# Division by shared row sums and the output projection at later ticks in a four-layer attention kernel

## The chip, the cores and the metric

The kernel runs on one core of one Trainium2 chip, in one launch, in fp32 throughout. The metric is device time in microseconds. The time before is the median of three runs, 2481.57 us (2477.61 to 2482.33).

## The reference, cut to what matters

The input is `x` of shape (4, 512, 32, 32): four images, each 512 channels by 1024 positions. Four layers follow each other. Layer 0 is attention with 8 heads of 64 channels, layer 1 is linear attention, layer 2 is attention with one head of 512 channels, layer 3 is attention with 4 heads of 128 channels after a group norm. Layers 0 and 3 are what the change touches. Both do this:

```python
attn = softmax(q @ k.T * scale)      # over 1024 keys
res  = attn @ v                      # per head
out  = res @ Wo.T + bo + x
```

The softmax is computed here without subtracting a maximum: exps are summed per row, the exps multiply the values as they are, and the product is divided by the row sum afterwards. That division, and the projection by `Wo` behind it, are what is moved.

## The kernel before, in words

`plain_path` is the path that runs. It goes layer by layer and image by image. For each image of layers 0 and 3, `project_qkv` makes q, k and v, and `attention` (L895) does the rest, with its output projection running on into the next image's `project_qkv`.

**Steps of `attention`.** The queries are halved into `qb` = 0, 1 (512 positions each). The channels are four chunks `g` = 0..3 of 128, which in layer 0 hold two heads each (`pair` is true) and in layer 3 one head. A step `(qb, g, i)` treats a part of the keys: 128 in layer 0 (8 steps per `g`), 256 in layer 3 (4 steps per `g`). `scores(n)` (L919) multiplies q and k into a PSUM tile `sc` (L924 in layer 0, L929 in layer 3), ScalarE takes the exp into a tile `pt` (L934; there are four `pt` buffers, so an exp waits until the values and the addition of the step four back are through), and VectorE adds the exps of a chunk into `sum` (L940 for the first two steps, L943 for each later one, L950 folds the halves in layer 3). `values(n - 2)` (L952) multiplies the exps of two steps back with v into PSUM tiles `acc` (L960 in layer 0, L975 in layer 3). At the last step of a chunk the product is copied into the tile `ot` (L970 and L971 in layer 0, where two PSUM tiles are joined; L983 in layer 3). `ot` has one buffer, `acc` has four.

**Shared row sums.** Chunks are grouped (`shared`, L912 to L916). In layer 0 the groups are two chunks each, three groups per image; the last two chunks of an image have their sums made singly by `sum_rows` (L985, matmuls at L992). In layer 3 the groups are the four chunks of `qb` = 0 and the first three of `qb` = 1. When a group is complete, `sum_shared` (L1004) multiplies its `sum` tiles with ones (L1011), so that each head's row sums lie in a few partitions, takes one reciprocal for the whole group (L678, with two reductions at L681), and sends the quotients by DMA to a small DRAM tile (L1023) and from there, broadcast over partitions, into the tile `rds` (L1026; two transfers in layer 0, one in layer 3). `normalise` (L1035) multiplies one chunk of `ot` with its quotients on VectorE (L1039) and adds the output bias to `x` on ScalarE (L1042).

**The output projection.** `project_out` (L1050) multiplies `ot` with `wo` by seven block products instead of eight. Its lead is the first product, a ScalarE copy of that PSUM tile (L1091), and four additions and subtractions of blocks of `ot` on VectorE (`sum_inputs`, L686 to L689). It returns three further pieces, `second`, `third` and `fourth`, each with two products (four matmuls of 128x256 each, all at L1072) and additions into `x` or the scratch tile `ou` (L1080, L1102). `second` accumulates onto the PSUM tile of the lead; `fourth` accumulates onto the two tiles of `third`. In layer 3 each finished block of `x` is stored by a DMA (L1085).

**What sets the order.** TensorE's order is the program's order, written out by hand. On the other engines a planner orders the instructions by its own model of costs; `tc.issue_after(ins)` tells it to place what is issued inside behind `ins`, and `soon()` gives a higher priority. Within the loop of steps, `later` is a first-in-first-out list of `[ticks, function]`: `tick()` (L651), called after each `values`, lowers all counts by one and runs what has come to zero from the front of the list. Layer 0 has two steps per turn of the loop (`per` = 2): two `scores`, then two times values and a tick.

Before the change, in layer 0 a complete group gets one entry due after one tick, which does `sum_shared` and straight after it `normalise` of both chunks. In layer 3 `sum_shared` is called ahead of the last `values` of the group, and `normalise` right behind that. `project_out`'s lead and three pieces for `qb` = 0 are due after 5, 6, 7, 8 ticks in layer 0 and after 4, 5, 5, 6 in layer 3. For `qb` = 1, whose last chunk isn't shared, the counts are one (layer 0) or two (layer 3) lower, and the change leaves them alone.

Of the kernel before, what the change touches and what calls it, by code (L numbers as in the profile page):

```python
# [15 lines left out]
ALU = mybir.AluOpType  # L16
# [458 lines left out]
def plain_path(ctx: ExitStack, tc: tile.TileContext, d: dict, out: bass.AP, count):  # L475
# [11 lines left out]
    nc = tc.nc  # L487
# [11 lines left out]
    def acc_tile():  # L499
        return ps_acc.tile([P, TB], F32, tag="acc", name="acc")  # L500

    def two_tile(name):
        return ps_sc.tile([P, 2, TB], F32, tag="sc", name=name)

    def row_tile(name):
        return work.tile([P, TB], F32, tag="row", bufs=3, name=name)

    def pt_tile(name):
        return work.tile([P, 2, TB], F32, tag="pt", bufs=4, name=name)

    def sum_tile(name):
        return work.tile([P, 2, TB], F32, tag="sum", bufs=2, name=name)

    def many_tile(name):
        return work.tile([P, NC, TB], F32, tag="many", name=name)
# [129 lines left out]
    later, pieces = [], []  # L645
# [5 lines left out]
    def tick():  # L651
        for item in later:
            item[0] -= 1
        while later and later[0][0] <= 0:
            later.pop(0)[1]()
# [13 lines left out]
    def flush():  # L669
        while later:  # L670
            later.pop(0)[1]()
        while pieces:
            pieces.pop(0)()


    def invert(rd, ps):

        nc.vector.reciprocal(rd, ps)  # L678
        n, m = next(unit), rd.shape[0]
        for i, t in enumerate((ps, rd)):  # L680
            closing[:] = [nc.vector.tensor_reduce(tops[:m, i, n : n + 1], t, AX.X, ALU.max).ins]  # L681
# [213 lines left out]
    def attention(b, q, key, v, heads, scale, wo, os, bo, hooks={}, last=False, end=None, plain=False):  # L895
# [6 lines left out]
        pair = hd < P  # L902
# [5 lines left out]
        pts, accs, rds, outs, ots, exps = {}, {}, {}, {}, {}, []  # L908
# [5 lines left out]
        else:  # L914
            shared = [[(qb, g) for g in range(NC - qb)] for qb in range(NTB)]
        group_of = {u: us for us in shared for u in us}  # L916
        parts_of = {}

        def scores(n):  # L919
            qb, g, i = steps[n]  # L920
            ps = two_tile("sc")
            if pair:
                for h, s in itertools.product(range(2), range(2)):
                    nc.tensor.matmul(  # L924
                        ps[half(h), s, :], lhsT=key(g, i)[half(s), half(h)],
                        rhs=q[qb][half(s), g, :], start=True, stop=True,
                    )
            for s in range(0 if pair else 2):
                nc.tensor.matmul(  # L929
                    ps[:, s, :], lhsT=key(g, 2 * i + s), rhs=q[qb][:, g, :], start=True, stop=True  # L930
                )
            pt = pt_tile("pt")
            with soon():
                exps.append(nc.scalar.activation(pt, ps, AF.Exp, scale=scale).ins)  # L934
            pts[n] = pt
            us = group_of.get((qb, g), [])
            if i == 1:
                acc = many_tile("sum")[:, :2, :] if pair and g % 2 and us else sum_tile("sum")
                accs[qb, g] = acc
                nc.vector.tensor_tensor(acc, pts[n - 1], pt, ALU.add)  # L940
            elif i > 1:
                acc = accs[qb, g]
                nc.vector.tensor_tensor(acc, acc, pt, ALU.add)  # L943
            if i == nsteps - 1 and not pair:
                total = acc[:, 0, :]
                if us:
                    if g == 0:
                        parts_of[qb] = many_tile("sums")
                    total = accs[qb, g] = parts_of[qb][:, g, :]
                nc.vector.tensor_tensor(total, acc[:, 0, :], acc[:, 1, :], ALU.add)  # L950
# [53 lines left out]
        def sum_shared(us):  # L1004

            heads = [(u, s) for u in us for s in range(2 if pair else 1)]
            n = P // 4
            ps = acc_tile()
            for k, (u, s) in enumerate(heads):
                acc = accs[u]  # L1010
                nc.tensor.matmul(  # L1011
                    ps[k * n : (k + 1) * n, :], lhsT=ones[:, :n],
                    rhs=acc[:, s, :] if pair else acc, start=True, stop=True,
                )
            m = len(heads) * n
            rd = row_tile("rd")
            invert(rd[:m], ps[:m])
            spread = work.tile([P, NC, TB], F32, tag="rds", name="rds")

            home = dram.tile(  # L1020
                [len(heads), TB], F32, tag=f"quotients{len(heads)}", bufs=2, name="quotients"
            )
            nc.sync.dma_start(home, rd[0:m:n])  # L1023
            for s in range(2 if pair else 1):
                to = spread[half(s) if pair else slice(0, P)]
                nc.sync.dma_start(  # L1026
                    to[:, : len(us), :],
                    home[s :: 2 if pair else 1].partition_broadcast(to.shape[0]),
                )
            for i, u in enumerate(us):  # L1030
                accs.pop(u)
                rds[u] = spread[:, i, :]
            return us

        def normalise(qb, g):  # L1035
            rd = rds.pop((qb, g))
            o = ots[qb][:, g, :]
            source = outs.pop((qb, g))[0] if (qb, g) in outs else o
            nc.vector.tensor_tensor(o, source, rd, ALU.mult)  # L1039
            xv = x[:, g, bass.ts(qb, TB)]  # L1040
            with tc.issue_after(exps[-1]):
                nc.scalar.activation(xv, xv, AF.Identity, bias=bo[:, g : g + 1])  # L1042
# [108 lines left out]
        for m in range(0, len(steps) + 2, per):  # L1151
            for n in range(m, m + per):
                if n < len(steps):
                    scores(n)
            for n in range(m, m + per):
                if n >= 2:
                    qb, g, i = steps[n - 2]
                    final = i == nsteps - 1

                    us = group_of.get((qb, g))  # L1160
                    closes = us and (qb, g) == us[-1]
                    if final and not pair and closes:
                        sum_shared(us)
                    elif final and not pair and not us:
                        sum_rows(qb, g)
                    values(n - 2)
                    tick()
                    if final and pair and closes:
                        later.append(
                            [1, lambda us=us: [normalise(*u) for u in sum_shared(us)]]  # L1170
                        )
                    elif final and pair and not us:
                        later.append([1, lambda qb=qb, g=g: (sum_rows(qb, g), normalise(qb, g))])
                    elif final and closes:
                        for u in us:
                            normalise(*u)
                    elif final and not pair and not us:
                        normalise(qb, g)
                    if n - 2 == len(steps) - 1 and end is not None:
                        flush()  # L1180
                        end_program(qb)
                    elif final and g == NC - 1 and plain and qb == NTB - 1:
                        later.append([2 * per + 1, lambda qb=qb: project_out_plain(qb)])
                    elif final and g == NC - 1:
                        rest = []
                        lead, *others = (4, 5, 6, 7) if pair else (2, 3, 3, 4)

                        wait = (1 if pair else 2) if us else 0
                        later.append(
                            [lead + wait, lambda qb=qb, rest=rest: rest.extend(project_out(qb))]  # L1190
                        )
                        for i in others:
                            later.append([i + wait, lambda rest=rest: rest.pop(0)()])
                if parts:
                    parts.pop(0)()
                if n in hooks:
                    parts.extend(hooks[n]())
# [444 lines left out]
    with tc.manual_schedule(engines={mybir.EngineType.PE}):  # L1642
# [95 lines left out]
        for b in range(B):  # L1738
# [20 lines left out]
            pair = lambda t, i: t[:, 2 * i : 2 * i + 2, :]  # L1759
# [145 lines left out]
```

## Time and profile before

| | |
|---|---|
| runs, median of 3 | 2481.57 us (2477.61 to 2482.33) |
| profiled execution, its own time | 2483.01 us |
| its span, first to last instruction | 2481.2 us |
| mean granted TensorE clock | 0.998 |
| layer 0, attention of image 0 (79 to 212 us): PE, DVE, ACT busy | 128.22, 99.62, 70.35 of 133 us |
| layer 3, attention of image 0 (1704 to 1830 us): PE, DVE, ACT busy | 126.00, 64.36, 45.24 of 126 us |
| L1039 divisions by `rds`, 128x512, two in a row | 1.29 us |
| L943 additions of exps, 128x1024 | 1.23 us each |
| transfers `quotients`, `rds` | 24 of 256 KB and 4 of 1024 KB for `rds` |

A row of the timeline gives the start in us from the span's start, the duration in us, the engine, the line, the operation, the tiles written and read, and how many instructions in a row it merges. Where the engine was idle before it, the idle time and what ended it follow in brackets. PE rows are pipelined: one row's end overlaps the next one's start, so waits on PE are better read from start to start. Each fp32 matmul shows as two rows.

### The profile page before, as it was taken

Reading aid. Unit: us, or ns where it says so; the run is one execution under the profiler, and the core shown is the slowest. Engines: PE = TensorE matmul, PEld = TensorE weight load, DVE = VectorE, ACT = ScalarE, POOL = GpSimd, SP = SyncE. Lnnn points to the kernel's source line nnn. Section 1 sums busy time; section 2 is a strip of 40 time slices with the busy share of each in tenths; the row PEclk is TensorE's granted clock in tenths of the full one; section 3 lists DMA queues with packets and bytes.
Section 4 is the critical chain, followed back from the end, with each engine's and each line's share of the span. In section 5 each row is a group of like instructions: output and inputs, shape, how many; then the busy total and the mean of one; then the engine's idle time right before and its main releaser. Section 6 shows DMA issues by size and latency. Waiting matters only on the chain.

```text
span 2481.2 us, 24717 instructions
## 1 busy us (share of the span) xinstructions
PE 2449.9 (99%) x10122; PEld 1222.9 (49%) x10122; DVE 1530.0 (62%) x1822; ACT 708.9 (29%) x867; POOL 252.5 (10%) x240
## 2 busy tenths in 40 slices
PE   9999999999999999999999999999999999999998
PEld 4444544454445443554644546446556455555644
DVE  3577567856775678657676684763554454455344
ACT  1444244414441444211120301102320421332132
POOL 4001100110011000300302112021011001002000
PEclk9999999999999999999999999999999999999999
DMA  5000020002000301010101002110010001000001
GB/s 183 10 10 9 5 77 10 10 5 77 10 9 5 128 18 60 0 72 0 68 0 68 5 0 85 51 68 18 26 38 34 17 30 51 1 34 30 1 22 44
DMA packets 28064, 86.25 MB, mean 35 GB/s; under 512 B 2396, under 2 KB 10076, under 8 KB 25384
## 3 DMA queue, kind: packets, MB, share of 16 engines
q1 hardware_dynamic: 27944, 84.61, 9.5%
q8 instruction: 81, 1.33, 0.2%
q14 instruction: 39, 0.32, 0.0%
HBM read 58.23 MB, written 25.32 MB: 34 GB/s over the span
## 4 chain that ended last, share of the span: by engine, by line
PE 90%; DVE 5%; DMA 3%; ACT 1%; issue 1%; SPq 0%; DVEq 0%; ACTq 0%
PE acc L706 20%; PE acc L827 11%; PE acc L975 9%; PE sc L929 9%; PE acc L834 8%; PE acc L1072 6%; PE acc L1300 6%; PE sc L924 6%; PE acc L960 5%; PE acc L1261 2%; DVE sum L943 2%; DMA rds<-quotients 2%; DVE rd L678 2%; PE feat L641 1%; ACT pt L934 1%; PE acc L641 1%
## 5 line engine op out<-in xcount | busy, mean ns | idle before, releaser
L934 ACT ACTIVATE pt<-sc 128x1024 f32<-128x1024 f32 x384 | 381.1, 1024 | 605.6 <-PE sc L929 333.7
L943 DVE TENSOR_TENSOR sum<-sum,pt 128x1024 f32<-128x1024 f32 x256 | 314.4, 1228 | 149.3 <-ACT pt L934 139.0
L960 PE MATMUL acc<-pt,v 64*64 64x512 f32 x2048 | 260.1, 594 | 0.0
L924 PE MATMUL sc<-q,k 64*64 64x512 f32 x2048 | 254.1, 595 | 3.5 <-ACT pt L934 3.5
L975 PE MATMUL acc<-pt,v 128*128 128x512 f32 x512 | 240.8, 594 | 0.0
L929 PE MATMUL sc<-q,k 128*128 128x512 f32 x512 | 239.8, 593 | 0.0
L694 POOL TENSOR_TENSOR ws<-wqkv 128x256 f32<-128x256 f32 (+1 forms) x40 | 40.7, 1017 | 1332.4 <-PE acc L992 560.8
L706 PE MATMUL acc<-t,ws 128*128 128x512 f32 x384 | 173.9, 593 | 0.0
L975 PEld LDWEIGHTS acc<-pt,v 128*128 128x128 f32 x512 | 96.6, 190 | 125.3 <-issue 124.4
L940 DVE TENSOR_TENSOR sum<-pt 128x1024 f32<-128x1024 f32 x64 | 77.9, 1217 | 124.4 <-ACT pt L934 124.4
L929 PEld LDWEIGHTS sc<-q,k 128*128 128x128 f32 x512 | 96.8, 190 | 112.8 <-issue 90.8
L924 PEld LDWEIGHTS sc<-q,k 64*64 64x64 f32 x2048 | 78.8, 134 | 147.6 <-issue 130.4
L960 PEld LDWEIGHTS acc<-pt,v 64*64 64x64 f32 x2048 | 79.7, 133 | 143.5 <-issue 140.4
L706 PEld LDWEIGHTS acc<-t,ws 128*128 128x128 f32 x384 | 72.5, 190 | 86.6 <-issue 84.7
L678 DVE RECIPROCAL rd<-acc 128x512 f32<-128x512 f32 (+1 forms) x24 | 80.5, 3353 | 39.2 <-PE acc L1011 39.2
L745 ACT COPY v<-acc 128x512 f32<-128x512 f32 x24 | 14.1, 587 | 288.0 <-PE acc L827 288.0
L1072 PE MATMUL acc<-ot,wo 128*128 128x256 f32 x336 | 80.5, 382 | 7.5 <-DVE ot L1039 7.5
L827 PE MATMUL acc<-ws,t 128*128 128x256 f32 x384 | 87.3, 379 | 0.0
L834 PE MATMUL acc<-qs,w 128*128 128x512 f32 x192 | 86.6, 593 | 0.0
L834 PE MATMUL acc<-q,ln 128*128 128x512 f32 x192 | 85.8, 593 | 0.0
L745 ACT COPY q<-acc 128x512 f32<-128x512 f32 x40 | 23.5, 587 | 208.5 <-PE acc L706 208.5
L1072 PEld LDWEIGHTS acc<-ot,wo 128*128 128x128 f32 x336 | 62.8, 190 | 38.2 <-issue 23.5
(326 smaller groups left out, 3514.6 us busy)
## 6 DMA issues: line engine op xcount, KB each, us to landing
home<-x SPq DMA_DIRECT2D x8, 2048.0 KB
x<-home SPq DMA_DIRECT2D x8, 2048.0 KB
out<-x SPq DMA_DIRECT2D x32, 256.0 KB
x<-in_x SPq DMA_DIRECT2D x3, 2048.0 KB
rds<-quotients SPq DMA_DIRECT2D x24, 256.0 KB
rds<-quotients SPq DMA_DIRECT2D x4, 1024.0 KB
wo<-in_wo SPq DMA_DIRECT2D x3, 1024.0 KB
w<-in_w SPq DMA_DIRECT2D x1, 3072.0 KB
```

The lines of the kernel that those rows point to most:

```text
L678: nc.vector.reciprocal(rd, ps)
L706: nc.tensor.matmul(ps, lhsT=w[:, m, :], rhs=x[:, m, :], start=start, stop=stop, skip_group_check=True)
L827: nc.tensor.matmul(ps[:, bass.ts(r, C // 2)], lhsT=x[:, m, bass.ts(2 * o + r, P)], rhs=w[:, m, :], start=(start and r == 0), stop=stop, sk ...
L834: nc.tensor.matmul(ps, lhsT=x[:, m, bass.ts(o, P)], rhs=w[:, m, :], start=start, stop=stop, skip_group_check=True,)
L924: nc.tensor.matmul(ps[half(h), s, :], lhsT=key(g, i)[half(s), half(h)], rhs=q[qb][half(s), g, :], start=True, stop=True,)
L929: nc.tensor.matmul(ps[:, s, :], lhsT=key(g, 2 * i + s), rhs=q[qb][:, g, :], start=True, stop=True)
L934: exps.append(nc.scalar.activation(pt, ps, AF.Exp, scale=scale).ins)
L943: nc.vector.tensor_tensor(acc, acc, pt, ALU.add)
L960: nc.tensor.matmul(outs[qb, g][r][half(s), :], lhsT=v[i // 2][half(r), i % 2, g * P + s * hd : g * P + (s + 1) * hd], rhs=pt[half(r), s, : ...
L975: nc.tensor.matmul(outs[qb, g][0], lhsT=v[j // 2][:, j % 2, bass.ts(g, P)], rhs=pt[:, s, :], start=(j == 0), stop=(j == NT - 1),)
L1072: nc.tensor.matmul(ps[i][:, bass.ts(o, n)], lhsT=w[:, m, bass.ts(o, P)], rhs=t[:, m, :], start=(start and m + o == 0), stop=(stop and m == ...
L1300: nc.tensor.matmul(ps[i, o], lhsT=w[m][:, bass.ts(o, P)], rhs=t[m], start=(start and m == 0), stop=(stop and m == 3), skip_group_check=True,)
```

## The change

`sum_shared` no longer leads straight into `normalise`. A new function, `normalise_shared`, does the divisions and bias additions of a group, placed behind the latest addition of exps that has been issued at that time (the new list `adds` holds them all). In layer 0 `sum_shared` stays due after one tick and the divisions are due after five. In layer 3 the divisions are due three ticks after the group is complete instead of at once. `project_out` for `qb` = 0 is due after 6, 7, 8, 8 ticks in layer 0 instead of 5, 6, 7, 8, and in layer 3 all four pieces are due after 4 ticks instead of 4, 5, 5, 6.

```diff
-        parts_of = {}
+        parts_of, adds = {}, []
...
-                nc.vector.tensor_tensor(acc, pts[n - 1], pt, ALU.add)
+                adds.append(nc.vector.tensor_tensor(acc, pts[n - 1], pt, ALU.add).ins)
             elif i > 1:
                 acc = accs[qb, g]
-                nc.vector.tensor_tensor(acc, acc, pt, ALU.add)
+                adds.append(nc.vector.tensor_tensor(acc, acc, pt, ALU.add).ins)
...
-            return us
+
+        def normalise_shared(us):
+
+            with tc.issue_after(adds[-1]):
+                for u in us:
+                    normalise(*u)
...
                     if final and pair and closes:
-                        later.append(
-                            [1, lambda us=us: [normalise(*u) for u in sum_shared(us)]]
-                        )
+                        later.append([1, lambda us=us: sum_shared(us)])
+                        later.append([5, lambda us=us: normalise_shared(us)])
...
                     elif final and closes:
-                        for u in us:
-                            normalise(*u)
+                        later.append([3, lambda us=us: normalise_shared(us)])
...
-                        lead, *others = (4, 5, 6, 7) if pair else (2, 3, 3, 4)
-
-                        wait = (1 if pair else 2) if us else 0
+
+
+                        if pair:
+                            lead, *others = (6, 7, 8, 8) if us else (4, 5, 6, 7)
+                        else:
+                            lead, *others = (4, 4, 4, 4) if us else (2, 3, 3, 4)
                         later.append(
-                            [lead + wait, lambda qb=qb, rest=rest: rest.extend(project_out(qb))]
+                            [lead, lambda qb=qb, rest=rest: rest.extend(project_out(qb))]
                         )
                         for i in others:
-                            later.append([i + wait, lambda rest=rest: rest.pop(0)()])
+                            later.append([i, lambda rest=rest: rest.pop(0)()])
```

## The prediction

> **What bounds the kernel now.** I began with the page's busy table: TensorE is the bound, and little is left on it.
>
> ```profile
> PE 2449.9 (99%) x10122; PEld 1222.9 (49%) x10122; DVE 1530.0 (62%) x1822; ACT 708.9 (29%) x867; POOL 252.5 (10%) x240
> ```
>
> So an edit pays only if PE waits less. The second view was the list of waits, kept to PE (total us, times, longest):
>
> ```profile
> PE acc L1072 <- DVE ot L1039: 7.5, 4, 2.0
> PE acc L992 <- DVE sum L943: 4.8, 4, 1.4
> ...
> PE sc L924 <- ACT pt L934: 3.5, 8, 0.6
> PE acc L992 <- DVE ot L971: 2.4, 4, 0.6
> PE acc L1072 <- DVE oi L687: 1.1, 4, 0.3
> ```
>
> L1039 is the division that the change moves. Counts of four are one per image, all in layer 0's attention. Third, the timeline of VectorE after the third shared group of image 0, where the quotients come back by DMA:
>
> ```profile
> 192.10 2.55 DVE L943 TENSOR_TENSOR sum<-sum,pt 128x1024 f32<-128x1024 f32 x2
> 197.77 1.29 DVE L1039 TENSOR_TENSOR ot<-ot,rds 128x512 f32<-128x512 f32 x2 [3.13 <-DMA rds<-quotients]
> 198.98 1.22 DVE L943 TENSOR_TENSOR sum<-sum,pt 128x1024 f32<-128x1024 f32 x1
> ...
> 200.72 1.22 DVE L943 TENSOR_TENSOR sum<-sum,pt 128x1024 f32<-128x1024 f32 x1
> 201.85 1.22 DVE L940 TENSOR_TENSOR sum<-pt 128x1024 f32<-128x1024 f32 x1
> 202.99 0.68 DVE L971 TENSOR_TENSOR ot<-ot,acc 128x512 f32<-128x512 f32 x1
> ```
>
> VectorE stands 3.13 us in front of the division with two additions behind it whose exps were finished long before. PE in the same stretch:
>
> ```profile
> 199.67 1.04 PE L960 MATMUL acc<-pt,v 64*64 64x512 f32 x8
> 202.08 1.04 PE L992 MATMUL acc<-sum,ones 64*64 64x512 f32 x2 [1.38 <-DVE sum L943]
> 203.73 0.66 PE L992 MATMUL acc<-sum,ones 64*64 64x512 f32 x3 [0.60 <-DVE ot L971]
> ```
>
> Fourth, granted clock by stretch (start:end, length, then busy us of PE, PEld, DVE, ACT, POOL, then PEclk):
>
> ```profile
> 205.00:207.00 2.00, 2.00 (x16) 0.79 (x12) 1.97 (x3) 0.59 (x1) 1.59 (x2) 0.50 0.00 0
> 454.00:456.00 2.00, 2.00 (x24) 0.67 (x20) 1.97 (x3) 1.01 (x2) 2.00 (x3) 1.00 0.02 4
> ```
>
> After that stall image 0 runs at half clock; image 1, at the same place, doesn't. Images 0 and 2 took 13.80 and 13.86 us from L992 to the first L706, images 1 and 3 both 12.17. Last, layer 3 (from 1705 us), by the same timeline, has no PE stall at all.
>
> **What the Trainium skill says.** "TensorE: Matmul & The Clock Gate", Architectural detail: ScalarE and VectorE are strict FIFO. The trace agrees: ready additions stood 3.13 us behind L1039. Same page, Part 1, the HAM clock gate: an idle window of about 3.4 us, free-running, halves the clock. The trace agrees roughly: 0.50 for about 3.4 us, in two images of four with the same stalls. "DMA: Bandwidth & Descriptors", Anatomy of one DMA: about 2 us fixed, mostly completion. The quotients' two chained transfers took 6.7 us here (issue 191.08, division 197.77). "PSUM — Partial Sum Buffer", PSUM bank collisions: a bank that another engine reads must be guarded against a matmul's write; no row of before has PE stopped by it.
>
> **The change part by part.** I measure stalls start to start: 16 rows of 64x512 take 1.72 us when nothing stops them, so 8 take 0.86. The instruction order of the built changed kernel gives the new places. SP and POOL keep theirs row for row; no DMA changes place in a queue. `sum_shared` with its reciprocal and three transfers (two in layer 3) stays put; only the two to four divisions with as many bias additions (L1042, ScalarE), and `project_out`, move.
>
> (a) Layer 0, first group (PE near 127.5). VectorE's order becomes four additions, two divisions, instead of two, two, one, one. Additions: 118.21 + 4 x 1.23 = 123.1; quotients at 123.9; 0.8 us of waiting remains and nobody needs what is behind it before 125. The exps that waited for those additions (126.43, 128.17) run at the usual beat, 125.2. PE's 8 rows at 127.51 took 1.73 instead of 0.86: excess 0.87, in the other images 0.84, 0.61, 0.87. Gain 3.2.
>
> (b) Second group and `project_out` (PE 146 to 169). Lead, second and third pieces come a tick later; third and fourth run together. The division still ends its first half at 153.9, its second at 154.5. PE: scores from 146.76, values to 150.2, lead to 152.1, scores to 153.8, 8 rows of values to 154.7, then the second piece. So it arrives after the division; before, it stood ready at 152.2. Excess of the 8 rows at 151.37: 1.82, and 2.19, 2.20, 2.16 for the others, less 0.1 each for the change of tile size that rows without a wait show: 8.0. The wait for L687 (1.1 in all) goes too: L687 ends at 155.1 and is wanted at 156.6. One interruption of the 64-wide matmuls fewer saves about 0.2 per image, 0.8. Gain 9.9. What is late next: the third piece wants a PSUM buffer that VectorE frees at about 158.3; PE comes at 159.5. Cover 1.2 us.
>
> (c) Third group (PE near 200). Four additions: 192.10 to 197.0; division 197.8 to 199.1; L686 to 199.7; L940 to 200.8; L971 to 201.4. The first wait of L992 (sum ready 197.0, PE there at 200.6) goes: 1.55 + 1.46 + 1.46 + 1.01 less 0.1 each = 5.1. Its second, for L971, was 1.43 per image start to start; PE now comes earlier, and L971 at 201.4 leaves 0.7. Gain 0.7 x 4 = 2.9. Together 8.0.
>
> (d) The half clock after (c): PE would idle 0.7 instead of about 3 us there, so I take it away: 13.80 + 13.86 - 2 x 12.17 = 3.3. Bounds: 0 if it stays, 3.3 at most.
>
> (e) Layer 3. The divisions keep their place on VectorE, behind the additions as before: nothing gained. Four bias additions (2.7 us) move on ScalarE behind three exps and L983's copy, into gaps of 2.4 us between exps; an exp slips by some 0.2 us with 3 us of cover. Two additions and L950 move behind the adds of `project_out`; their sums are wanted tens of us later. But all four pieces are now one block of 56 matmul rows (12.0 us), without the scores and values that stood between lead and second:
>
> ```profile
> 1779.05 1.89 PE L1072 MATMUL acc<-ot,wo 128*128 128x256 f32 x8
> 1780.78 1.88 PE L929 MATMUL sc<-q,k 128*128 128x512 f32 x4
> 1782.50 1.88 PE L975 MATMUL acc<-pt,v 128*128 128x512 f32 x4
> 1784.21 1.89 PE L1072 MATMUL acc<-ot,wo 128*128 128x256 f32 x8
> ```
>
> The second piece accumulates onto the bank that L1091 copies after the lead. ScalarE did that from 1780.98 to 1781.57. That was covered by 3.4 us of scores and values; with the cover gone, PE, done issuing at 1780.77, goes on at about 1781.65: 0.9 per image, 3.6 in all. Behind it on PE stands everything. From below: 0, if the copy didn't hold the bank; from above, about 2 us per image, if the two later reuses of a bank wait as well. I worked these out: VectorE's reads end 0.8 us before PE wants the banks. I take 0.9. The stores in layer 3 (four of 256 KB per image) keep their order, issue up to 5 us earlier, and nobody waits for them.
>
> Sum: 3.2 + 9.9 + 8.0 + 3.3 - 3.6 = 20.8 us, against the profiled execution's own 2483.0 us (span 2481.2): 2462.2. The median of the runs is 2481.6, 1.4 below that execution; a run with fewer half-clock stretches has less to win and ends at the same place. I forecast 2462 us.
>
> **Rivals.** *The wait only moves.* VectorE still waits 0.4 to 0.8 us in front of each division, and what stands behind it has little slack; half of (b) and (c) comes back as waits for L940, L971 or a PSUM buffer. For: L971 already stops PE. Against: the slacks of 0.9 to 1.2 us in (b). Gain 3.2 + 5.0 + 4.0 + 1.7 - 3.6 = 10.3: 2473 us. *Layer 3's block serialises* (slower): each of the seven products stands before the read of its bank, with drain, operation and signal (0.2 + 0.7 + 0.05, from these rows) exposed, 6.6 us, and PE, chopped like that, falls to half clock for a stretch as in (d), 1.7. That is 8.3 per image. It decides from (3.2 + 9.9 + 8.0 + 3.3) / 4 = 6.1 us per image on. Then 2483.0 + 4 x 8.3 - 24.4 = 2492. For: PE order admits nothing else between. Against: before already had 24 rows without a break (1785.94 to 1791.12) at full pace, and only the lead's bank is reused at once. *The change does nothing*: the tie is only an order for the planner. But the built order shows VectorE's rows moved in all twelve places of layer 0. 2482 us.
>
> **How the numbers follow.** Forecast 0.72; the wait moves 0.17; serialised block 0.08; nothing 0.03. Range: low 2456 has (e) at 0 and all of L992's second wait gone (3.6 + 2.8 below 2462); high 2474 takes in the moved wait, or (d) staying with the upper bound of (e) and no gain on L971. What lies above is the last two cases, about 0.11 with the forecast's own tail. Faster by over 0.2% (5 us, about what a measurement of this kernel can tell from no change): 0.87; within: 0.05; slower: 0.08.
>
> **What would show it.** In the changed profile: PE's wait for L1039's successor near zero; L992 waiting for L971 alone, about 0.6 us idle or less; L924's waits for exps near 127 gone; no stretch at 0.50 clock after L992; in layer 3, four waits of PE's L1072 successor for ScalarE's copy, near 0.7 us each, and none for VectorE. The prediction is wrong if the block in layer 3 costs over 2 us per image or if L992 still waits for L943.

## The result, and the profile after

The changed kernel takes 2459.34 us (median of four runs, 2458.34 to 2460.14); the kernel before, measured beside it, took 2481.18 us (four runs, 2477.61 to 2482.33). The ratio is 0.9914, interval 0.9897 to 0.9931: faster by 0.9%. The profiled execution took 2459.86 us with a span of 2458.1 us, against 2483.0 and 2481.2. The forecast was 2462 us.

TensorE still bounds the kernel. From the page of the changed kernel, its busy table and the first line of the chain that ended last (shares of the span by engine):

```profile
PE 2441.7 (99%) x10122; PEld 1226.2 (50%) x10122; DVE 1532.8 (62%) x1822; ACT 706.4 (29%) x867; POOL 253.2 (10%) x240
...
PE 97%; DVE 1%; DMA 1%; ACT 0%; issue 0%; SPq 0%; DVEq 0%
```

Before, PE had 90% of that chain, VectorE 5% and DMA 3%. The same matmuls now follow each other with less in between. PE's list of waits after (total us, times, longest):

```profile
PE acc L706 <- DMA wqkv<-in_wqkv: 4.3, 1, 4.3
PE acc L1077 <- ACT ou L1096: 2.7, 4, 0.7
PE sc L924 <- ACT pt L934: 1.1, 4, 0.3
PE acc L1126 <- DVE ot L1044: 0.8, 1, 0.8
PE lnsums L1555 <- DVE s L1549: 0.7, 1, 0.7
PE acc L1077 <- ACT pt L934: 0.4, 1, 0.4
```

L1039 is L1044 now, L1072 is L1077, L1091 is L1096. The 7.5 us of L1072 for the division are gone from the list, and so is L992. What is new is L1096, four times 0.68 us: the price paid in layer 3.

In front of the projection's second piece, PE in image 0 before, then after:

```profile
151.37 1.09 PE L960 MATMUL acc<-pt,v 64*64 64x512 f32 x8
154.05 1.97 PE L1072 MATMUL acc<-ot,wo 128*128 128x256 f32 x8 [1.59 <-DVE ot L1039]
```

```profile
152.44 1.04 PE L960 MATMUL acc<-pt,v 64*64 64x512 f32 x8
153.41 1.99 PE L1077 MATMUL acc<-ot,wo 128*128 128x256 f32 x8
```

In image 1 PE still stops there, which is the last line of the list. VectorE and PE:

```profile
393.99 1.29 DVE L1044 TENSOR_TENSOR ot<-ot,rds 128x512 f32<-128x512 f32 x2 [1.63 <-DMA rds<-quotients]
394.83 1.96 PE L1077 MATMUL acc<-ot,wo 128*128 128x256 f32 x8 [0.41 <-ACT pt L934]
```

The list puts the stop down to an exp that ended at 394.71. But the quotients came late here (VectorE waited 1.63 us for them, in the other eleven groups 0.2 to 0.6), and the first of the two divisions ended at 394.68, only 0.03 us before. Without the exp PE would most likely have stood for the division almost as long. So the wait for the division is hidden by a small margin and not abolished.

VectorE and then PE at the third group of image 0, for comparison with the stretch near 197 us in the prediction:

```profile
188.00 5.21 DVE L943 TENSOR_TENSOR sum<-sum,pt 128x1024 f32<-128x1024 f32 x4
193.78 1.29 DVE L1044 TENSOR_TENSOR ot<-ot,rds 128x512 f32<-128x512 f32 x2 [0.58 <-DMA rds<-quotients]
...
195.72 1.22 DVE L940 TENSOR_TENSOR sum<-pt 128x1024 f32<-128x1024 f32 x1
196.85 0.68 DVE L971 TENSOR_TENSOR ot<-ot,acc 128x512 f32<-128x512 f32 x1
```

```profile
195.57 1.04 PE L960 MATMUL acc<-pt,v 64*64 64x512 f32 x8
196.43 1.81 PE L992 MATMUL acc<-sum,ones 64*64 64x512 f32 x5
```

All four additions stand ahead of the division, the wait for the quotients is 0.58 us instead of 3.13, and PE's L992 begins 0.86 us after the eight rows before it, without a gap (its later rows still come late; see (c) below). The stretch that ran at half clock in images 0 and 2 is at full clock, here images 0 and 2, 1.6 us behind the first L992 (PEclk is the third number from the end):

```profile
198.03:202.43 4.40, 4.40 (x48) 1.61 (x43) 4.26 (x4) 2.53 (x3) 3.50 (x4) 1.00 0.00 0
...
680.10:684.50 4.40, 4.40 (x48) 1.65 (x44) 4.26 (x4) 2.53 (x3) 3.54 (x4) 1.00 0.02 4
```

In layer 3 the projection is one block, and PE stops once in it, in front of the piece that accumulates onto the bank being copied. PE and then ScalarE, image 0:

```profile
1752.32 1.89 PE L1077 MATMUL acc<-ot,wo 128*128 128x256 f32 x8
1754.88 1.99 PE L1077 MATMUL acc<-ot,wo 128*128 128x256 f32 x8 [0.68 <-ACT ou L1096]
1756.71 5.34 PE L1077 MATMUL acc<-oi,os 128*128 128x256 f32 x24
```

```profile
1754.25 0.58 ACT L1096 COPY ou<-acc 128x512 f32<-128x512 f32 x1 [2.36 <-PE acc L1077]
```

The copy ends at 1754.83 and the next row starts at 1754.88. From start to start the eight rows of the lead took 2.56 us instead of 1.73.

To compare the two traces step by step I used PE's own marks: the starts of L1011 (row sums of a group), L992 and L706. The gain of each stretch, summed over the four images:

| stretch | predicted | measured | per image |
|---|---|---|---|
| (a) L1011 of group 1 to group 2 | 3.2 | 3.5 | 0.94, 0.90, 0.67, 0.99 |
| (b) L1011 of group 2 to group 3 | 9.9 | 10.8 | 2.54, 2.46, 2.92, 2.88 |
| (c) + (d) from there to the next image's L706 (image 3: its second L992) | 11.3 | 11.8 | 3.74, 2.23, 3.67, 2.15 |
| (e) layer 3, first L1011 to second | -3.6 | -3.8 | -0.94 each |
| sum | 20.8 | 22.3 | |

The spans differ by 23.1 us, the medians by 21.8. Of the 0.8 us of the spans that the table lacks, 0.6 lies ahead of the first attention (its first L924 starts at 78.75 instead of 79.37), where the change alters nothing; I count that as variation from execution to execution.

### The profile page after: what moved, and what is told of

Read it like the earlier page. It is cut to its first block, busy times and chain, and to the rows that moved or that the text cites. A ratio compares the mean times of both kernels' runs of the same rounds, so it can differ in the third digit from the quotient of the medians.

```text
span 2458.1 us, 24712 instructions
## 1 busy us (share of the span) xinstructions
PE 2441.7 (99%) x10122; PEld 1226.2 (50%) x10122; DVE 1532.8 (62%) x1822; ACT 706.4 (29%) x867; POOL 253.2 (10%) x240
## 4 chain that ended last, share of the span: by engine, by line
PE 97%; DVE 1%; DMA 1%; ACT 0%; issue 0%; SPq 0%; DVEq 0%
PE acc L706 20%; PE acc L827 11%; PE acc L975 9%; PE sc L929 9%; PE acc L960 8%; PE sc L924 8%; PE acc L834 8%; PE acc L1077 7%; PE acc L1306 6%; PE acc L1267 2%; PE feat L641 1%; PE acc L641 1%; PE acc L1011 1%; PE upd L1510 1%; PE acc L1444 1%; PE xt L1415 1%
## 5 line engine op out<-in xcount | busy, mean ns | idle before, releaser
L934 ACT ACTIVATE pt<-sc 128x1024 f32<-128x1024 f32 x384 | 379.2, 1022 | 540.1 <-PE sc L929 304.0
L943 DVE TENSOR_TENSOR sum<-sum,pt 128x1024 f32<-128x1024 f32 x256 | 314.4, 1228 | 150.0 <-ACT pt L934 137.3
L924 PE MATMUL sc<-q,k 64*64 64x512 f32 x2048 | 249.9, 591 | 1.1 <-ACT pt L934 1.1
L694 POOL TENSOR_TENSOR ws<-wqkv 128x256 f32<-128x256 f32 (+1 forms) x40 | 41.4, 1036 | 1313.8 <-PE acc L992 539.9
L706 PE MATMUL acc<-t,ws 128*128 128x512 f32 x384 | 173.9, 593 | 0.0
L924 PEld LDWEIGHTS sc<-q,k 64*64 64x64 f32 x2048 | 79.1, 133 | 140.6 <-issue 130.5
L706 PEld LDWEIGHTS acc<-t,ws 128*128 128x128 f32 x384 | 72.5, 190 | 86.6 <-issue 85.1
L1077 PE MATMUL acc<-ot,wo 128*128 128x256 f32 x336 | 80.6, 383 | 3.1 <-ACT ou L1096 2.7
L736 DVE TENSOR_TENSOR v<-acc,v 128x512 f32<-128x512 f32 x72 | 49.5, 688 | 51.5 <-PE acc L827 51.3
```

The costliest lines, as they stand in the source:

```text
L706: nc.tensor.matmul(ps, lhsT=w[:, m, :], rhs=x[:, m, :], start=start, stop=stop, skip_group_check=True)
L924: nc.tensor.matmul(ps[half(h), s, :], lhsT=key(g, i)[half(s), half(h)], rhs=q[qb][half(s), g, :], start=True, stop=True,)
L943: adds.append(nc.vector.tensor_tensor(acc, acc, pt, ALU.add).ins)
L1077: nc.tensor.matmul(ps[i][:, bass.ts(o, n)], lhsT=w[:, m, bass.ts(o, P)], rhs=t[:, m, :], start=(start and m + o == 0), stop=(stop and m == ...
```

## The experiments

The theory: in layer 0 the gain is VectorE's order (additions ahead of the wait for the quotients) together with a projection that comes late enough for the division; in layer 3 nothing but the copy's lost cover counts. The rivals: the layer 3 part or the block's length costs something else; the tie alone or the delay alone does the work; the half clock comes from another stall.

The ratios are against runs of the kernel before that were measured beside each group of experiments: 2481.64 us (41 runs) for the first four, 2482.71 (25 runs) for the next four, 2480.35 (9 runs) for the last two. The kernel before thus moves by 2 us from group to group. Differences of about 1 us between medians of different groups, the changed kernel's own among them, decide nothing; where they matter I go by the traces.

**1. The change in layer 0 alone.** Layer 3 gets its old ticks and its immediate division.

```diff
-                        later.append([3, lambda us=us: normalise_shared(us)])
+                        for u in us:
+                            normalise(*u)
...
-                            lead, *others = (4, 4, 4, 4) if us else (2, 3, 3, 4)
+                            lead, *others = (4, 5, 5, 6) if us else (2, 3, 3, 4)
```

> The changed kernel with layer 3 put back to the old ticks and the old place of the divisions. Theory (the gain is made in layer 0 alone, layer 3's unbroken block costs 0.94 us per image): 2459.3 - 3.8 = 2455.5 us, and PE's four waits for the copy of the lead are gone. Rival (fewer interruptions in layer 3 are part of the gain): 2459 us or more.

Measured: 2455.71 us (2455.47 to 2456.74), ratio 0.9899 (0.9884 to 0.9914). The wait for L1096 is gone from PE's list. The change is better without its part in layer 3, by 3.6 us.

**2. The change in layer 3 alone.** Layer 0's divisions follow `sum_shared` in the same entry and the projection has its old ticks.

```diff
-                        later.append([1, lambda us=us: sum_shared(us)])
-                        later.append([5, lambda us=us: normalise_shared(us)])
+                        later.append([1, lambda us=us: (sum_shared(us), [normalise(*u) for u in us])])
...
-                            lead, *others = (6, 7, 8, 8) if us else (4, 5, 6, 7)
+                            lead, *others = (5, 6, 7, 8) if us else (4, 5, 6, 7)
```

> The kernel before with only layer 3's part of the change. Theory: 2481.2 + 3.8 = 2485.0 us, with four waits of PE for the copy of the lead, 0.7 us each, and nothing else moved. Rival (layer 3 gains): below 2481 us.

Measured: 2485.42 us (2481.12 to 2488.93), ratio 1.0015 (1.0009 to 1.0022). Layer 3 alone makes the kernel slower by 3.8 us, as (e) says: 55.43 us from L1011 to L1011 in each image, 54.48 before.

**3. The delay without the tie.**

```diff
-            with tc.issue_after(adds[-1]):
-                for u in us:
-                    normalise(*u)
+            for u in us:
+                normalise(*u)
```

> The changed kernel without the tie: same ticks, but the planner is free to put the divisions where it likes. It puts them behind two additions again, as before. Theory (the two additions more ahead of the divisions make (a) and (c), the later tick of the projection makes part of (b)): (a) 3.5 and (c) 11.8 lost, of (b) 10.8 about 6 kept, so 2459.3 + 3.5 + 11.8 + 4.8 = 2479 us; PE waits for exps near 127 and for L943 at L992 as before. Rival (the later ticks make the gain): 2459 to 2462 us.

Measured: 2478.62 us (2476.84 to 2481.9), ratio 0.9989 (0.9982 to 0.9995). The planner puts each division behind two additions again, though it is issued later, and VectorE waits 3.2 us for the quotients as before. Two of PE's waits:

```profile
PE acc L992 <- DVE sum L943: 5.3, 4, 1.5
...
PE acc L1076 <- DVE x L1084: 3.8, 4, 1.2
```

The first is the old stall. The second is the one that the prediction named as late next in (b): the third piece wants a PSUM buffer that VectorE frees. In the changed kernel it has cover; here VectorE is late and it has none. By the marks the later ticks alone still gain 6.6 us in (b); (a) and (c) gain nothing.

**4. The tie with the projection at its old ticks.**

```diff
-                            lead, *others = (6, 7, 8, 8) if us else (4, 5, 6, 7)
+                            lead, *others = (5, 6, 7, 8) if us else (4, 5, 6, 7)
```

> The changed kernel with layer 0's projection at its old ticks 5, 6, 7, 8. Theory: (a) and (c) stay, and in (b) the second piece stands in front of the division again, since the quotients' transfer ends no earlier: 1.6 to 2.2 us per image, so 2459.3 + 8 = 2467 us (2464 to 2469). Rival (the tie alone makes (b) too): 2459 to 2461 us.

Measured: 2467.61 us (2467.47 to 2468.48), ratio 0.9947 (0.9933 to 0.996), 8.3 us above the changed kernel. The first line of PE's waits:

```profile
PE acc L1077 <- DVE ot L1044: 6.6, 4, 1.7
```

By the marks, (b) takes 2.05, 1.63, 2.04 and 1.98 us longer per image than in the changed kernel, so the later ticks carry 7.7 of its 10.8 us (the 8.3 us between the medians hold some 0.6 from elsewhere). With VectorE's new order alone (b) gains 3.1 us, and PE still stands in front of the division.

**5. Layer 3 with the cover restored.** The divisions stay delayed; the three later pieces come one tick behind the lead.

```diff
-                            lead, *others = (4, 4, 4, 4) if us else (2, 3, 3, 4)
+                            lead, *others = (4, 5, 5, 5) if us else (2, 3, 3, 4)
```

> The changed kernel, but in layer 3 the second, third and fourth piece of the projection come one tick behind the lead again (4, 5, 5, 5), so that scores and values stand between the lead and the piece that accumulates onto the bank under copy. Theory (the copy's cover is what layer 3 lost): the wait of the projection for the copy is gone from PE's list, and the time is that of the changed kernel less 3.4 us, about 2455.9. Rival (the longer unbroken block or the bias additions that moved are the cost): no less than 2458.5.

Measured: 2456.71 us (2456.04 to 2458.37), ratio 0.9897 (0.9882 to 0.9912): 2.6 us below the changed kernel, 0.8 less than forecast. The wait for the copy is gone and L1011 to L1011 is 54.48 us again. In the profiled execution 0.5 us came back in one image of layer 3 with a wait of the next image's projection for VectorE (L706 for L738, 0.3 us, in the list), and 0.6 us lies behind the last row sums, where I found no single cause.

**6. The unbroken block, with two products swapped.** In the second piece the product that goes to a bank of its own comes first.

```diff
+                if not pair:
+                    mult(6, os[1], t[1])
                 mult(1, w(0, 1), inputs(1, 0), start=False)
                 finish(0, 0, 1, xv(0, 0))
-                mult(6, os[1], t[1])
+                if pair:
+                    mult(6, os[1], t[1])
                 add(6, d)
```

> The changed kernel with its unbroken block in layer 3, but inside the second piece the product that goes to a bank of its own comes ahead of the one that accumulates onto the bank under copy (for both query halves). Nothing but that order changes, so 8 rows of matmuls stand over the copy. Theory: the wait for the copy is gone with the block left whole, about 2455.9. Rival (the block's length is the cost): about 2459.

Measured: 2456.05 us (2455.82 to 2458.23), ratio 0.9897 (0.9882 to 0.9912), 3.3 us below the changed kernel. PE's rows in the block:

```profile
1751.84 1.89 PE L1077 MATMUL acc<-ot,wo 128*128 128x256 f32 x8
1753.56 1.89 PE L1077 MATMUL acc<-oi,os 128*128 128x256 f32 x8
1755.29 1.89 PE L1077 MATMUL acc<-ot,wo 128*128 128x256 f32 x8
```

They start every 1.72 to 1.73 us: the copy lies beside the second row. L1011 to L1011 is 54.48 us again. The block has as many rows as in the changed kernel, and its bias additions lie where they lay there, so neither costs anything that can be measured; the copy alone did.

**7. The third group's divisions behind the join too.** What is left of the stall at L992 has the division and its wait standing ahead of L971. Built on experiment 1.

```diff
-                    nc.vector.tensor_tensor(o, o, upper, ALU.add)
+                    adds.append(nc.vector.tensor_tensor(o, o, upper, ALU.add).ins)
...
-                        later.append([5, lambda us=us: normalise_shared(us)])
+                        later.append([8 if us[-1][0] else 5, lambda us=us: normalise_shared(us)])
```

> The kernel with the change in layer 0 alone, with the divisions of the third group moved on behind the join of the last chunk's product as well, so that VectorE does the first addition of the next chunk and the join ahead of the division. Theory (what is left of the stall before the row sums of the last chunks is the division's 0.58 us of waiting and its 1.3 us, standing ahead of the join): the four remaining excesses of 0.3 to 0.6 us go, 2453.5 to 2454. Rival (the join is bound by the copy on ScalarE and the last product itself): nothing gained, 2455.7. A loss would say that the projection now waits for the later division.

Measured: 2460.19 us (2458.79 to 2460.81), ratio 0.991 (0.9897 to 0.9924): 4.5 us above experiment 1 (3.5 by the two traces), and neither theory nor rival. At the first L992 the theory holds: PE runs through, and the next image's first L706 comes 11.26 us after the values ahead of L992 instead of 12.22. Against this trace, what was left of the stall in experiment 1 is 0.95, 0.87, 1.17 and 0.55 us per image, and in the changed kernel 1.20, 0.93, 1.17 and 0.57, more than the 0.3 to 0.6 us that I expected. But the second L992, for the last chunk, now waits for its additions (`PE acc L992 <- DVE sum L943`, 4.8 us, three times). VectorE and then GpSimd after the division, image 0:

```profile
196.95 0.69 DVE L686 TENSOR_TENSOR oi<-ot 128x512 f32<-128x512 f32 x1
197.56 3.42 DVE L943 TENSOR_TENSOR sum<-sum,pt 128x1024 f32<-128x1024 f32 x2
200.91 0.68 DVE L998 TENSOR_TENSOR rs<-rs,acc 128x512 f32<-128x512 f32 x1
```

```profile
197.50 0.74 POOL L694 TENSOR_TENSOR ws<-wqkv 128x256 f32<-128x256 f32 x1 [157.20 <-PE acc L992]
198.19 1.71 POOL L696 TENSOR_TENSOR ws<-wqkv 128x256 f32<-128x256 f32 x1
199.86 1.71 POOL L695 TENSOR_TENSOR ws<-ws,wqkv 128x256 f32<-128x256 f32 x1
```

Two additions take 3.42 us instead of 2.55, and a sum of weights 1.71 instead of 0.72. GpSimd's sums for the next image are released by L992, which comes earlier, and here fall onto VectorE's additions. Image 3 has no such sums, and there the wait is absent: three times, not four. "SBUF — State Buffer", section "SBUF: two separate sides", says that VectorE (with two inputs in SBUF) and GpSimd share one pair of ports under an exclusive lock, held for a whole instruction. The rows agree: each starts while one of the other engine runs and grows by nearly what is left of it. The first addition starts with 0.68 us of L694 left and takes 0.52 more than its 1.23; L696 starts with 1.12 us of that addition left and takes 0.99 more. In experiment 1, image 0, L694 collides too (1.73 us), but there GpSimd alone loses: the two additions took 2.55 us together.

**8. The tie without the delay.** The divisions are issued in the same tick as `sum_shared`.

```diff
-                        later.append([5, lambda us=us: normalise_shared(us)])
+                        later.append([1, lambda us=us: normalise_shared(us)])
```

> The change in layer 0 alone, with the divisions tied behind the latest addition but issued in the same tick as the row sums, as before the change, and the projection at its new ticks. Theory (the tie reaches only what has been issued, so two additions and not four come ahead of the division, and the waits in front of the row sums stay): as the kernel with the delay but without the tie, less what layer 3 costs, 2474 to 2480, with L992 waiting 5 us in all for the additions. Rival (the tie is what matters and the delay is not): 2455.7.

The expectation is wrong in one point: the kernel that ran keeps the change in layer 3 too, so its partner is experiment 3, at 2478.6 us. Measured: 2480.21 us (2478.38 to 2483.14), ratio 0.999 (0.9984 to 0.9997). The tie reaches only additions that have been issued, so two stand ahead of the division:

```profile
190.82 2.55 DVE L943 TENSOR_TENSOR sum<-sum,pt 128x1024 f32<-128x1024 f32 x2
196.39 1.29 DVE L1044 TENSOR_TENSOR ot<-ot,rds 128x512 f32<-128x512 f32 x2 [3.02 <-DMA rds<-quotients]
```

L992 waits 4.9 us for the additions. Neither the tie nor the delay gives VectorE's order; only both together do.

**9. Experiment 7 with GpSimd's sums held back.** A copy of one column of the last sum stands ahead of them on GpSimd.

```diff
...
+            mark = small.tile([P, 1], F32, tag="mark", name="mark")
+            with tc.issue_after(nc.gpsimd.tensor_copy(mark, latest.pop()[:, 0, :1]).ins):
+                return block_sums(w)
...
```

> The kernel of the join experiment (third group's divisions behind the join), with GpSimd's first sums of weights for the next image held back until the last addition of exps is done, by a copy of one column of that sum ahead of them; nothing else moves. Theory (the loss came from GpSimd's sums of weights running beside VectorE's additions and slowing both): the two additions behind the division take 1.23 us each again, the wait for the last addition falls from 1.6 to at most 0.6 us, and the time is 2454 to 2455.5. Rival (the later division alone makes VectorE late): 2459 to 2460.

Measured: 2456.84 us (2455.91 to 2457.43), ratio 0.9904 (0.9889 to 0.992): 3.4 us below experiment 7, yet 1.1 above experiment 1, where a small gain was expected. VectorE in the same stretch:

```profile
198.92 2.55 DVE L952 TENSOR_TENSOR sum<-sum,pt 128x1024 f32<-128x1024 f32 x2
...
207.10 5.21 DVE L952 TENSOR_TENSOR sum<-sum,pt 128x1024 f32<-128x1024 f32 x4
```

The additions are back at 1.23 us each (L952 is L943 here). PE at the second L992 (L1003 here), in experiment 1, in experiment 7 and in this one:

```profile
211.32 1.09 PE L992 MATMUL acc<-sum,ones 64*64 64x512 f32 x8
...
211.97 1.59 PE L992 MATMUL acc<-sum,ones 64*64 64x512 f32 x8 [1.59 <-DVE sum L943]
...
212.45 1.59 PE L1003 MATMUL acc<-sum,ones 64*64 64x512 f32 x8 [0.72 <-ACT q L745]
```

The wait is shorter by about 0.87 us than in experiment 7 in each of three images, 2.6 us in all: that much was the collision. The 0.72 us that are left, more than the 0.6 that I allowed, are put down to a copy that ended at 212.36, but the additions ended at 212.31, only 0.05 us earlier: without the copy PE would wait as well. From the first L992, PE comes 0.95 us earlier than in experiment 1 and the additions end 0.53 us later; experiment 1 had 0.83 us of slack there. By the marks 0.79 us is lost at this L992. And after the wait its eight rows take 1.52 us instead of 1.02 until the next row starts, in this experiment as in 7; no run shows why. So in image 0 1.3 us is lost where 0.95 was won. Of the 2.0 us by which the span is longer than that of experiment 1, 1.3 lie ahead of the first attention, which neither edit touches; the two kernels are about equal. In this stretch VectorE's own work has become the bound: while it stays as it is, what is won at the first L992 is given back at the second.

**10. The third group of layer 0 alone.** Groups 1 and 2, the projection and layer 3 are as before the change.

```diff
+                        if not us[-1][0]:
+                            later.append([1, lambda us=us: (sum_shared(us), [normalise(*u) for u in us])])
+                        else:
+                            later.append([1, lambda us=us: sum_shared(us)])
+                            later.append([5, lambda us=us: normalise_shared(us)])
```

> The kernel before, with only the third group's divisions of layer 0 moved as in the change; the first two groups, the projection and layer 3 as before. Theory (what I put on the third group: the wait for the additions, most of the wait for the join, and the half clock that followed in some images; 11.8 us by the two traces): 2469.5 to 2471, no half clock behind the row sums in any image, and the waits of the projection for the division left at 7 us. Rival (the half clock came from the second group's stall as much as from this one, or the groups' gains overlap): 2473 or more.

Measured: 2468.81 us (2468.58 to 2469.87), ratio 0.9955 (0.9941 to 0.9968): a gain of 11.5 us against the kernel before, where 11.8 was expected (the time is 0.7 us below the expected stretch, as the kernel before was low in this group too). PE still waits 7.0 us for the division in front of the projection, but no stretch behind L992 is at half clock in any image. Images 0 and 2:

```profile
201.74:206.14 4.40, 4.40 (x48) 1.65 (x44) 4.26 (x4) 2.53 (x3) 3.62 (x4) 1.00 0.00 0
...
689.80:694.20 4.40, 4.40 (x48) 1.62 (x44) 4.26 (x4) 2.53 (x3) 3.67 (x4) 1.00 0.01 4
```

So the half clock belongs to the stall at L992 and not to the one at the projection. The seven other traces without that stall (the changed kernel's and those of experiments 1, 4, 5, 6, 7 and 9) have no half clock in layer 0 either.

## Why the prediction was right, step by step

The mechanism was right in each of its five steps, and the time fell 2.7 us below the forecast. Of that, 1.5 us are in the steps. The rest is not theirs: 0.8 us of the spans' difference lies outside the marks, and the median is 0.5 us below the profiled execution.

*(a), the first group: 3.5 against 3.2.* VectorE waits 0.32 us for the quotients instead of the 0.8 that I worked out, which nobody on PE's path needed. The rows that had an excess of 0.61 to 0.87 us have none: the sixteen of L924 that start at 126.88 in image 0 take 1.71 us, and the stretch is 28.6 us long in every image.

*(b), the second group and the projection: 10.8 against 9.9.* PE comes to the second piece after the division, and in three images it doesn't wait; image 1, where the quotients came late, lost 0.4 us. Experiment 4 shows that the ticks carry 7.7 us of it, the term that I had at 8.0. The wait for L687 is gone as well. The order on VectorE gave 3.1 us by itself, where my two smaller terms, from few rows, came to 1.9; I did not settle which of them was short.

*(c), the third group: 8.4 against 8.0, and one term right by luck.* The first wait of L992 is gone, and gave 5.5 us instead of 5.1: from L1011 of the third group to L992 takes 14.78 us, and took 16.33, 16.25, 16.24 and 15.80. The 0.1 that I took off per image was not there to take. For the second wait I had 1.43 per image, of which 0.7 would be left. Where PE runs through (experiments 7 and 9), L992 to L706 takes 10.41 us; before it took 12.10 in image 1, at full clock. So the wait had cost 1.69, and 1.20, 0.93, 1.17 and 0.57 are left. The gain of 2.9 us that I wrote down is what was measured, but both of its sides were about 1 us too small in all. Experiments 7 and 9 show what happens when that rest is taken too: it comes back at the next L992.

*(d), the half clock: 3.4 against 3.3.* Gone, as forecast. From the first row of L992 to the first L706, images 0 and 2 took 13.80 and 13.79 us before, image 1 at full clock 12.10, so the two stretches cost 1.7 us each. (The prediction has 13.86 and 12.17 for images 2 and 1, and an L706 behind image 3, where L641 stands; that moves the term by less than 0.1.) Experiment 10 ties it to the stall at L992.

*(e), layer 3: 3.8 against 3.6.* The wait is for the copy, 0.68 us idle and 0.94 per image from L1011 to L1011. The prediction says of the page that it cited, "PSUM — Partial Sum Buffer", that no row of before has PE stopped by such a read. Its own list has two: L924 stops for the exp L934, which reads `sc`, and L992 for L971, which reads an `acc` tile. What is new is a stop for a copy of the bank that the next product accumulates onto. Experiments 1, 2 and 6 put the loss at 3.3 to 3.8 us; experiment 5 won back 2.6 of it and lost some elsewhere. Experiment 6 rules out the block's length.

Of the rivals, *the wait only moves* is what happens when one half of the change is missing (experiments 3, 4 and 8) or when one goes a step further (7 and 9). The changed kernel stays clear of it, but for 0.4 us in image 1, because additions and ticks move together. *Layer 3's block serialises* would have needed 6.1 us per image; it cost 0.94.

The best version that ran is experiment 1, at 2455.71 us: 3.6 us below the changed kernel. Experiment 6 keeps layer 3's block and is at 2456.05.

## What to carry to other kernels

An operation that waits for a DMA belongs behind the ready work on its in-order engine, and its consumer has to come late enough for it. Parts of this gave 2.5 us (the tie without the delay), 3.0 (the delay without the tie) and 14 (both, with the consumer at its old ticks); all of it gave 22. Each of these has layer 3's loss in it; without that, all of it gave 26. When pieces of matmuls are pushed together, look for the one whose PSUM bank another engine reads, and put a product with a bank of its own in between. Before taking the last tenths of a stall, work out the slack of what comes next on every engine, and what an earlier PE releases on the others.

## What the runs showed of the hardware that I had not expected

A stall of about 3 us at L992 (1.55 and 1.69 us, as in (c)), in two parts with a few matmuls between them, was followed by a stretch of half clock in some images and not in others of the same execution: in the traces of before and of experiments 2, 3 and 8, which all have it, in 2, 1, 3 and 1 images of four. Each lasts 3.41 us and costs 1.7 (13.80 less 12.10 in (d)). The stall at the projection, up to 2.0 us in one piece, was never followed by one.

Much of the scatter between runs goes with it. In the four traces the mean granted clock of the execution goes with the count of such stretches: 0.998 with two, 0.999 with one, 0.997 with three, 0.999 with one. And the time goes with the clock: of the 41 runs of before in the first group, 7 at a mean clock of 0.999 took 2479.3 us on average, 28 at 0.998 took 2481.6 and 6 at 0.997 took 2484.4. The runs of kernels with the stall spread by 4.8 to 8.8 us (21 to 41 runs) and their clock goes down to 0.995; the 35 runs of kernels without it all have 0.999 or 1.0, and spread by 1.0 to 2.4 us (four or five runs each; fewer runs show less spread, but the clock doesn't depend on their number). So this stall bought scatter with its loss.

A sum of weights on GpSimd (128x256) took 0.72 us by itself and 1.71 us beside additions on VectorE, and an addition of 1.23 us took up to 1.75. Beside VectorE's reciprocal, which has one input, GpSimd's sums took 0.72 to 0.73 us in experiment 9.
